# Sparse attention block on one core: tile ends taken in fewer half groups, the mean factor put closer behind its power, and the heaviest tiles summed on the matmul engine alone

## The chip, the cores and the metric

The kernel runs on one core of a Trainium2 chip. The metric is the device time of one execution in microseconds (us), lower is better; the time before is the median of three runs. The trace of one further execution was taken with the hardware profiler.

## The reference, cut to what matters

There are 4096 rows of width 512. Each target row attends only to the source rows that its row of `adj` marks, a few tens at most, with 8 heads of 64.

```python
hs = layer_norm(x, ln1_scale, ln1_bias)
ht = layer_norm(h_target, ln1_scale, ln1_bias)
q = (ht @ Wq + bq).reshape(T, H, HD) / sqrt(HD)
k = (hs @ Wk + bk).reshape(S, H, HD)
v = (hs @ Wv + bv).reshape(S, H, HD)
logits = where(adj != 0, einsum('thd,shd->hts', q, k), NEG)
ctx = einsum('hts,shd->thd', softmax(logits), v).reshape(T, D)
ht = layer_norm(ht + ctx @ Wo + bo, ln2_scale, ln2_bias)
ff = gelu(ht @ W1) @ W2                  # W1: 512x2048, W2: 2048x512
x = _layernorm(x + ht + ff)
```

## The kernel before

**Stages.** Up to about 275 us the kernel projects all source rows to keys and values, stores them as rows of 1024 numbers in the DRAM table `kvd`, and turns the first half of `adj` into lists of neighbours, sorted by length. From then on each of 32 tiles holds 128 target rows of similar neighbour count. A tile's capacity is the longest list in it: the first tile has 11, then come pairs rising to 24; tile 15 has 39 and tile 17 has 38, each paired with a short tile (12 and 13); the pairs after that fall again. Tiles 0 to 15 belong to part 0, tiles 16 to 31 to part 1, whose lists are still built from `adj` while part 0 is being attended to.

**Attention** (`attention`, `values`, `by_scalar`). A tile's neighbours are taken in groups of S = 3 rows. GpSimd (POOL) issues one indirect DMA per row that gathers 128 key-and-value rows from `kvd` into a ring `kv` of 17 rows (20 for part 1). VectorE (DVE) multiplies keys with the query `tq` (L1242), reduces to logits `lg` (L1247) and multiplies two of the three value rows by the probabilities `p` (L1203); ScalarE (ACT) takes the exponential and scales the third row (L1226). From tile ADDS = 11 on DVE adds the second value row to the first (L1207), from tile DENSE = 21 on in every other group also the third (L1210). Each row that is left is added to the context `cps` by four transposing 128x128 matmuls on TensorE (PE, L1214). A slot of the ring comes free when these have read it.

**A tile's end** (`finish`) is a generator. Every group of three is two half groups; in each, `advance` takes one step (up to the next `yield`) of each tile end under way and of each `front` (the gather and projection of a coming tile's query). The steps of an end are: sums and reciprocals, transposes of them (L1117), the product with `cps` (L1122), the output projection `pa` (L1130, L1134), statistics, the variance plus epsilon (L680), its power -0.5 on POOL (L687), the mean factor `nm` (L692) and the normalisation (L1153), and the transposes into `h2T` (L1162, L1166). `turned` notes the tile whose `pa` has been issued, and a coming front may begin once the tile three before it is in `turned`.

**The feed-forward stream** (`feed`) handles one group of one or two tiles at a time. It waits for the group's `h2T`, multiplies by W1 (`pf`, L1348), applies gelu on ACT, multiplies by W2 into `po` (L1357), and hands the group to `end`, which does the last normalisation and stores the rows (L1303 to L1325). Its power also goes to POOL (L1312, L687), and its mean factor is L1318.

**Order.** `_weave` mixes the streams (attention, feed, the lists of part 1, loads of weights) by costs: the stream with the lowest clock goes next and its clock rises by the cost that it yields. Attention and feed have the same total cost per group, so feed runs at attention's pace and stays behind by as much as it was behind when its first `h2T` came. Every engine then runs its own instructions strictly in the resulting order, which the build may still shift a little for each engine.

**Loads of records.** `prefetch` loads a tile's record `rec` (neighbour numbers) on POOL's queue (L998), two tiles ahead.

Of the kernel before, what the change touches and what calls it, by code (L numbers as in the profile page):

```python
# [17 lines left out]
P = 128  # L18
# [360 lines left out]
RW = E0 + RE  # L379
# [64 lines left out]
def adj_resnorm_kernel(  # L444
# [33 lines left out]
    nc = tc.nc  # L478
# [4 lines left out]
    NT = N // P  # L483
# [12 lines left out]
    TILES = [t for g in groups for t in g]  # L496
# [4 lines left out]
    NA, NBT = len(CAPS_A), len(CAPS_B)  # L501
# [11 lines left out]
    recs_d = [dram.tile([n * P, RW], I32, name=f"rec{i}") for i, (_, n) in enumerate(PARTS)]  # L513
# [19 lines left out]
    with tc.tile_pool(name="keep", bufs=1) as keep:  # L533
# [17 lines left out]
        with ExitStack() as late:  # L551
# [126 lines left out]
            def shifted(pool, mv, n, name):  # L678
                ve = pool.tile([P, n], F32, name=name + "_ve")
                nc.vector.tensor_scalar_add(ve, mv[:, :, 1], EPS)  # L680
                return ve
# [13 lines left out]
            def stats(pool, src, mv, name):  # L695
                st = pool.tile([P, 6], F32, name=name + "_st")
                nc.vector.bn_stats(st, src)
                nc.vector.bn_aggr(mv, st)
# [290 lines left out]
            def prefetch(i):  # L989
                if i >= NT or i in recs:  # L990
                    return
                r0 = TILES[i][0]
                part = 1 if r0 >= PARTS[1][0] * P else 0
                assert part in done
                r0 -= PARTS[part][0] * P
                rec = sp.tile([P, E0 + MAXE], I32, name="rec", bufs=6)

                nc.gpsimd.dma_start(rec[:, :RW], recs_d[part][r0:r0 + P, :])  # L998
                recs[i] = rec

            def front(i, idle=0):
# [28 lines left out]
                for kc in range(KC):  # L1030
# [11 lines left out]
            SG = [(i, j0, min(S, cap - j0)) for i, (_, cap) in enumerate(TILES)  # L1042
                  for j0 in range(0, cap, S)]
# [5 lines left out]
                place.append(place[-1] + n)  # L1049

            begun_fronts, turned = set(range(EARLY)), set()
            first_b = next(k for k, (i, _, _) in enumerate(SG) if i >= NA)
            issued = [0]

            def step(gens, i):
# [40 lines left out]
            def finish(i, p, cps, group, hs, mv):  # L1096


                rec, tq, cap = recs[i], tqs.pop(i), TILES[i][1]

                nc.vector.scalar_tensor_tensor(p[:, :cap, :], rec[:, E0:E0 + cap].unsqueeze(2)
                                               .to_broadcast([P, cap, H]), 0.0, p[:, :cap, :],
                                               op0=ALU.is_gt, op1=ALU.mult)
                nc.vector.tensor_reduce(sums[:, i, :], p[:, :cap, :].rearrange("p j h -> p h j"),
                                        AX.X, ALU.add)
                ri = sp.tile([P, H], F32, name="ri")
                nc.vector.tensor_scalar_max(ri, sums[:, i, :], SUM_LO)
                nc.vector.reciprocal(ri, ri)
                rx = sp.tile([P, KC, P], F32, name="rb", bufs=1)
                rxf = rx.rearrange("p c t -> p (c t)")  # L1110
                nc.scalar.copy(rxf.rearrange("p (h d) -> p h d", h=H),
                               ri.unsqueeze(2).to_broadcast([P, H, HD]))
                yield
                yield
                prx = ps.tile([P, KC, P], F32, name="t", bufs=2)
                for c in range(KC):
                    nc.tensor.transpose(prx[:, c, :], rxf[:, c * P:(c + 1) * P], ident)  # L1117
                ct = sp.tile([P, KC, P], F32, name="rb", bufs=1)
                nc.scalar.copy(ct, prx)
                yield  # L1120
                yield
                nc.vector.tensor_mul(ct, cps, ct)  # L1122
                yield
                yield
                yield
                yield
                pa = ps.tile([P, D], F32, name="t", bufs=2)

                for c in range(KC):
                    nc.tensor.matmul(pa[:, c * P:(c + 1) * P], tq[:, D + c * P:D + (c + 1) * P],  # L1130
                                     ident, is_transpose=True, start=c == 0, stop=False,
                                     skip_group_check=True)
                for c in range(KC):
                    nc.tensor.matmul(pa, ct[:, c, :], wo[:, c, :], start=False,  # L1134
                                     stop=c == KC - 1, skip_group_check=True)
                turned.add(i)
                yield
                h = sp.tile([P, D], F32, name="h")
                nc.scalar.copy(h, pa)
                yield  # L1140
                stats(sp, h, mv[:, len(hs), :], "n2")
                hs.append(h)
                if len(hs) < len(group):
                    return
                nh = len(hs)
                ve = shifted(sp, mv[:, :nh, :], nh, "n2")
                yield
                rs = power(sp, mv[:, :nh, :], nh, "n2", ve)
                for _ in range(4):
                    yield  # L1150
                nm = negmean(sp, mv[:, :nh, :], rs, nh, "n2")
                for j, h in enumerate(hs):
                    nc.scalar.activation(h, h, AF.Identity, bias=nm[:, j:j + 1], scale=rs[:, j:j + 1])  # L1153
                yield
                yield
                w = len(hs) * P
                h2T = sp.tile([P, KC, 2 * P], F32, name="h2T")
                for k2 in range(KC // 2):
                    pt = ps.tile([P, 2, 2 * P], F32, name="t", bufs=2)
                    for k in range(2):  # L1160
                        for j, h in enumerate(hs):
                            nc.tensor.transpose(pt[:, k, j * P:(j + 1) * P],  # L1162
                                                h[:, (k2 * 2 + k) * P:(k2 * 2 + k + 1) * P], ident)
                    for k in range(2):
                        kc = k2 * 2 + k
                        nc.scalar.activation(h2T[:, kc, :w], pt[:, k, :w], AF.Identity,  # L1166
                                             bias=b2c[:, kc:kc + 1], scale=s2c[:, kc:kc + 1])
                h2Ts[GROUPS.index(group)] = h2T
# [17 lines left out]
            def attention():  # L1186
# [10 lines left out]
                def values(i, j0, n, kv, p, cps, after):  # L1197

                    m = n - 1 if n == S else n
                    v4 = kv[:, :m, D:].rearrange("p j (h d) -> p j h d", h=H)
                    nc.vector.tensor_tensor(v4, v4, p[:, j0:j0 + m, :].unsqueeze(3)  # L1203
                                            .to_broadcast([P, m, H, HD]), ALU.mult)
                    slots = list(range(n))
                    if m > 1 and i >= ADDS:
                        nc.vector.tensor_add(kv[:, 0, D:], kv[:, 0, D:], kv[:, 1, D:])  # L1207
                        slots.remove(1)
                        if n == S and i >= DENSE and j0 // S % 2:
                            nc.vector.tensor_add(kv[:, 0, D:], kv[:, 0, D:], kv[:, S - 1, D:])  # L1210
                            slots.remove(S - 1)
                    for j in slots:
                        for c in range(KC):
                            nc.tensor.matmul(cps[:, c, :], kv[:, j, D + c * P:D + (c + 1) * P], ident,  # L1214
                                             is_transpose=True, start=j0 + j == 0 and c == 0,
                                             stop=j0 + n == TILES[i][1] and j == slots[-1],
                                             skip_group_check=True)
                    if after is not None:
                        tails.append(after)
# [10 lines left out]
                k = 0  # L1230
                for group in GROUPS:
                    hs = []
                    mv = sp.tile([P, 2, 2], F32, name="mv2")
                    cost = 0.5 * UNIT * len(group) / 2 / sum(TILES[i][1] for i in group)
                    for i in group:
                        cps = ps.tile([P, KC, P], F32, name="cps", bufs=2)
                        while k < len(SG) and SG[k][0] == i:
                            _, j0, n = SG[k]
# [15 lines left out]
                            if pend:  # L1254
                                values(*pend.pop())
                                request(k)
# [41 lines left out]
            def end(group, xs, po):  # L1298
# [14 lines left out]
                yield  # L1313
                rs = power(sp, None, nt, "n3", ve)
                yield
                yield
                nm = sp.tile([P, nt], F32, name="n3_nm")
                nc.vector.tensor_mul(nm, sm[:, :nt, 0], rs)  # L1318
                yield
# [13 lines left out]
            def feed(g):  # L1333
# [5 lines left out]
                fb = 4 // nt  # L1339
                cost = UNIT * nt / 2 / (2 * FC // fb)  # L1340
                xs = []
# [62 lines left out]
            WAIT = 100.0  # L1404
            AHEAD = 4
            ADDS = 11
            DENSE = 21
            UNIT = 60.0

            ed = all_edges()  # L1410
# [107 lines left out]
```

## Time and profile before

| what | value |
|---|---|
| median of three runs | 1790.75 us (1786.41 to 1794.25) |
| profiled execution | 1796.99 us, its span 1795.3 us |
| PE busy | 1660.0 us, 92% of the span |
| DVE busy | 1434.3 us, 80% |
| ACT busy | 1238.7 us, 69% |
| POOL busy | 1049.6 us, 58% |
| last `pa` (tile 31) | starts at 1686.8 us |

The table's busy times are averages over stages with different limits, so the page's share of PE doesn't tell by itself what a change is worth: PE has long idle stretches up to about 1050 us and almost none after it. POOL's instructions that only issue a gather are counted as busy on it; the 0.3 us between two of them are not.

### The profile page before, as it was taken

The page shows a single profiled execution, that of the slowest core. Times are in us where ns is not written, and L with a number is a line of the kernel's source. Part 1 is how long each engine was busy: PE and PEld are TensorE (multiplying, and loading weights), DVE is VectorE, ACT ScalarE, POOL GpSimd, SP SyncE. Part 2 cuts the span into 40 slices and gives each one's busy share as a digit, 9 for nine tenths or more (in the row PEclk, how much of TensorE's full clock was granted, in tenths as well). Part 3 has the DMA queues.
Part 4 walks back from the last instruction along what each step waited for, and adds up shares of the span by engine and source line. Part 5 has one row for each costly group of instructions (what it writes and reads, how often), then busy time and mean ns, then how long its engine had stood idle before and what let it go on. Part 6 is the DMA issues. An engine that isn't in the chain of part 4 may idle for free. (4 is left out here: it accounts for less than half of the span.)

```text
span 1795.3 us, 22273 instructions
## 1 busy us (share of the span) xinstructions
PE 1660.0 (92%) x6746; PEld 1069.5 (60%) x6746; DVE 1434.3 (80%) x2475; ACT 1238.7 (69%) x3129; POOL 1049.6 (58%) x834
## 2 busy tenths in 40 slices
PE   7999985698999899988888899999999999999997
PEld 3444433576676666656556566666666666666664
DVE  6887786899997778968788999998989788979100
ACT  5776663588987686757667687877878778787211
POOL 1000156777656366777788787888777766671101
PEclk9999997799999999999989999999999999999998
DMA  9999978889878687676887677888776776772000
GB/s 354 373 390 361 348 249 317 335 307 353 306 239 295 229 280 270 220 232 208 275 285 254 235 270 270 310 291 292 259 260 235 248 243 228 240 266 75 24 18 26
DMA packets 140265, 460.99 MB, mean 257 GB/s; under 512 B 16500, under 2 KB 21704, under 8 KB 140136
## 3 DMA queue, kind: packets, MB, share of 16 engines
q0 software_dynamic: 96656, 342.51, 55.8%
q1 hardware_dynamic: 35664, 93.88, 14.6%
q10 hardware_dynamic: 7816, 23.08, 3.3%
q8 instruction: 56, 0.92, 0.2%
q14 instruction: 73, 0.60, 0.1%
HBM read 430.61 MB, written 28.79 MB: 256 GB/s over the span
## 5 line engine op out<-in xcount | busy, mean ns | idle before, releaser
L985 POOL DMA_INDIRECT kv<-kvd,rec x603 | 817.3, 1355 | 300.7 <-issue 133.2
L1348 PE MATMUL pf<-h2T,w 128*128 128x256 f32 (+1 forms) x2176 | 470.9, 370 | 1.4 <-ACT h2T L1166 1.4
L1357 PE MATMUL po<-w,gt 128*128 128x512 f32 x1024 | 464.5, 594 | 0.2 <-ACT gt L1351 0.2
L1348 PEld LDWEIGHTS pf<-h2T,w 128*128 128x128 f32 x2176 | 390.8, 192 | 66.3 <-issue 20.0
L1242 DVE TENSOR_TENSOR kv<-kv,tq 128x1536 f32<-128x1536 f32 (+2 forms) x211 | 352.5, 1678 | 57.5 <-DMA kv<-kvd,rec 49.9
L1226 ACT ACTIVATE kv<-kv,pa 128x64 f32<-128x64 f32 x1520 | 393.4, 339 | 4.3
L1247 DVE TENSOR_REDUCE lg<-kv 128x24 f32<-128x1536 f32 (+2 forms) x211 | 351.5, 1670 | 0.5
L1214 PE MATMUL cps<-ident,kv 128*128 128x128 f32 x1724 | 238.1, 284 | 73.0 <-DVE kv L1207 39.2
L1357 PEld LDWEIGHTS po<-w,gt 128*128 128x128 f32 x1024 | 188.4, 191 | 195.4 <-issue 192.9
L1214 PEld LDWEIGHTS cps<-ident,kv 128*128 128x128 f32 x1724 | 208.5, 146 | 154.1 <-DVE kv L1207 57.1
L1203 DVE TENSOR_TENSOR kv<-kv,p 128x1024 f32<-128x1024 f32 (+1 forms) x211 | 251.7, 1194 | 18.9 <-ACT p L1251 17.7
L687 POOL TENSOR_TENSOR n_rs<-n_ve,mhalf 128x2 f32<-128x2 f32 (+2 forms) x51 | 49.9, 978 | 317.6 <-DVE n_ve L680 148.7
L733 ACT ACTIVATE kv<-kv 128x1024 uint8<-128x1024 int32 x128 | 134.6, 1054 | 56.4 <-DMA kv<-in_adj_dram 21.4
L1351 ACT ACTIVATE gt<-pf 128x512 f32<-128x512 f32 x128 | 76.6, 598 | 97.4 <-PE pf L1348 90.2
L1351 ACT ACT_TABLE_LOAD x108 | 138.6, 1283 | 1.8
L1031 PE MATMUL t<-wq,tq 128*128 128x512 f32 x256 | 124.0, 628 | 5.0 <-ACT tq L1024 5.0
L947 PE MATMUL pq<-wv,h2T 128*128 128x512 f32 x256 | 118.3, 606 | 8.1 <-ACT kv L949 4.3
L947 PE MATMUL pq<-wk,h2T 128*128 128x512 f32 x256 | 118.9, 607 | 1.9 <-DMA wk<-in_L_gnn_Wk_dram 1.0
L1134 PE MATMUL t<-wo,rb 128*128 128x512 f32 x256 | 116.2, 592 | 0.0
L742 DVE MAX8 cand<-kv 128x8 uint16<-128x171 uint16 (+1 forms) x384 | 108.3, 326 | 6.9 <-remote 4.8
L1251 ACT ACTIVATE p<-lg 128x24 f32<-128x24 f32 (+2 forms) x179 | 39.4, 220 | 87.2 <-DVE lg L1247 79.8
L1207 DVE TENSOR_TENSOR kv<-kv 128x512 f32<-128x512 f32 x144 | 98.5, 685 | 0.4
(163 smaller groups left out, 1571.2 us busy)
## 6 DMA issues: line engine op xcount, KB each, us to landing
kv<-in_adj_dram SPq DMA_DIRECT2D x128, 512.0 KB
kvd<-tq ACTq DMA_DIRECT2D x23, 512.0 KB
kv<-kvd,rec POOLq DMA_INDIRECT x603
kv<-in_L_gnn_h_target_dram SPq DMA_DIRECT2D x32, 256.0 KB
kv<-in_x_dram SPq DMA_DIRECT2D x15, 512.0 KB
kvd<-kv ACTq DMA_DIRECT2D x9, 512.0 KB
w<-in_L_gnn_W_dram SPq DMA_DIRECT2D x4, 1024.0 KB
w<-in_L_gnn_W_dram ACTq DMA_DIRECT2D x4, 1024.0 KB
```

Source lines behind the costliest of these rows:

```text
L733: nc.scalar.activation(sg, a, AF.Sign, accum_out=dpart[:, i, h:h + 1])
L947: nc.tensor.matmul(pkv, hT[:, kc, j * P:(j + 1) * P], w[:, kc, :], start=kc == 0, stop=kc == KC - 1)
L985: issues[:] = [nc.gpsimd.indirect_dma_start(out=dst, out_offset=None, in_=table[:, :], in_offset=bass.IndirectOffsetOnAxis(ap=idx, axis=0) ...
L1031: nc.tensor.matmul(pq, hT[:, kc, :], wq[:, kc, :], start=kc == 0, stop=kc == KC - 1)
L1203: nc.vector.tensor_tensor(v4, v4, p[:, j0:j0 + m, :].unsqueeze(3) .to_broadcast([P, m, H, HD]), ALU.mult)
L1214: nc.tensor.matmul(cps[:, c, :], kv[:, j, D + c * P:D + (c + 1) * P], ident, is_transpose=True, start=j0 + j == 0 and c == 0, stop=j0 + n ...
L1226: newest[:] = [nc.scalar.mul(v, v, pa[:, hd:hd + 1]).ins]
L1242: nc.vector.tensor_tensor(kv[:, :n, :D], kv[:, :n, :D], tq[:, :D].unsqueeze(1).to_broadcast([P, n, D]), ALU.mult)
L1247: logits[:] = [nc.vector.tensor_reduce(lg[:, :n, :], kv[:, :n, :D].rearrange("p j (h d) -> p j h d", h=H), AX.X, ALU.add).ins]
L1348: nc.tensor.matmul(pf[:, k, :], w1[(f0 + k) // KC][:, kc, (f0 + k) % KC * P:((f0 + k) % KC + 1) * P], h2T[:, kc, :w], start=kc == 0, stop= ...
L1351: nc.scalar.activation(gt, pf, AF.Gelu_apprx_tanh)
L1357: nc.tensor.matmul(po[j], gt[:, k, j * P:(j + 1) * P], w2[(f0 + k) // KC][:, (f0 + k) % KC, :], start=False, stop=f0 + k == FC - 1, skip_g ...
```

## The change

The change has five edits.

1. For the first QUICK = 7 tiles an end's steps come after 1, 1, 1 and 1 half groups where they came after 2, 2, 4 and 2. All other tiles keep 2, 2, 4 and 2.
2. In every end, `nm` comes one half group after the power, not four.
3. In `end`, the mean factor comes one step after the power, not two.
4. Tiles with a capacity of at least HEAVY = 30 (15 and 17) have no additions on DVE: all three value rows of a group go to PE.
5. Records of part 1 are loaded by SyncE (SP) instead of POOL, except for the last four tiles.

An unused name, `first_b`, is removed as well.

```diff
-                nc.gpsimd.dma_start(rec[:, :RW], recs_d[part][r0:r0 + P, :])
+                (nc.sync if part and i < NT - 4 else nc.gpsimd).dma_start(rec[:, :RW], recs_d[part][r0:r0 + P, :])
...
                 rec, tq, cap = recs[i], tqs.pop(i), TILES[i][1]
+                slow = 0 if i < QUICK else 1
...
-                yield
-                yield
+                for _ in range(1 + 1 * slow):
+                    yield
                 prx = ps.tile([P, KC, P], F32, name="t", bufs=2)
...
                 nc.scalar.copy(ct, prx)
-                yield
-                yield
+                for _ in range(1 + 1 * slow):
+                    yield
                 nc.vector.tensor_mul(ct, cps, ct)
-                yield
-                yield
-                yield
-                yield
+                for _ in range(1 + 3 * slow):
+                    yield
                 pa = ps.tile([P, D], F32, name="t", bufs=2)
...
                 rs = power(sp, mv[:, :nh, :], nh, "n2", ve)
-                for _ in range(4):
-                    yield
+                yield
                 nm = negmean(sp, mv[:, :nh, :], rs, nh, "n2")
                 for j, h in enumerate(hs):
                     nc.scalar.activation(h, h, AF.Identity, bias=nm[:, j:j + 1], scale=rs[:, j:j + 1])
-                yield
-                yield
+                for _ in range(1 + 1 * slow):
+                    yield
...
-                    if m > 1 and i >= ADDS:
+                    if m > 1 and i >= ADDS and TILES[i][1] < HEAVY:
                         nc.vector.tensor_add(kv[:, 0, D:], kv[:, 0, D:], kv[:, 1, D:])
...
                 rs = power(sp, None, nt, "n3", ve)
                 yield
-                yield
                 nm = sp.tile([P, nt], F32, name="n3_nm")
...
+            HEAVY = 30
             DENSE = 21
+            QUICK = 7
```

More of the change, by code (lines that the diff above doesn't have):

```diff
@@ L1051, in adj_resnorm_kernel @@
             begun_fronts, turned = set(range(EARLY)), set()
-            first_b = next(k for k, (i, _, _) in enumerate(SG) if i >= NA)
             issued = [0]
```

## The prediction

> **What bounds the kernel now.** I read the busy time by stage first, then the end of PE's timeline for prices, then POOL's and DVE's timelines around the powers.
>
> ```profile
> core 0: us, PE busy (x) PEld busy (x) DVE busy (x) ACT busy (x) POOL busy (x), PEclk, DMA share, GB/s
> 340.00:605.00 265.00, 245.84 (x1185) 173.59 (x1184) 237.00 (x397) 210.04 (x554) 171.28 (x137) 0.97 0.82 290
> ...
> 776.00:945.00 169.00, 142.07 (x585) 96.92 (x585) 133.75 (x154) 110.03 (x308) 135.31 (x105) 0.91 0.76 253
> 945.00:1022.00 77.00, 67.34 (x292) 43.47 (x291) 68.82 (x70) 57.10 (x159) 62.35 (x39) 1.00 0.72 239
> ...
> 1050.00:1119.00 69.00, 67.27 (x289) 42.95 (x287) 67.53 (x70) 57.49 (x161) 56.46 (x40) 1.00 0.75 260
> 1119.00:1687.00 568.00, 562.05 (x2342) 374.81 (x2342) 483.14 (x597) 425.78 (x1099) 385.83 (x296) 1.00 0.70 236
> 1687.00:1795.00 108.00, 95.64 (x395) 62.89 (x393) 6.49 (x25) 18.02 (x34) 10.58 (x12) 0.96 0.06 21
> ```
>
> The cuts at 605, 945, 1022, 1050, 1119 and 1687 are where `pa` of tiles 7, 14, 15, 16, 17 and 31 runs, so 945 to 1022 and 1050 to 1119 are the two heavy tiles. After 1687 PE is alone with feed-forward matmuls that were left over. PE's timeline prices them:
>
> ```profile
> 1743.69 3.62 PE L1348 MATMUL pf<-h2T,w 128*128 128x256 f32 x16
> 1747.14 7.03 PE L1357 MATMUL po<-w,gt 128*128 128x512 f32 x16
> 1754.01 7.31 PE L1348 MATMUL pf<-h2T,w 128*128 128x128 f32 x64
> 1761.15 0.60 PE L1382 MATMUL po<-ident,h2T 128*128 128x128 f32 x4
> ```
>
> From start to start a record costs 0.216 us at 256 columns (3.45/16), 0.43 at 512 (6.87/16), 0.11 at 128 (7.14/64). At these prices the records of 1119 to 1687 add up to 566 of 568 us: **PE is the bound there**, and a matmul added or saved counts in full. Earlier PE has slack: 19.7 us of recorded idle in 340 to 605 (mainly 5.1 waiting for L1203 at 341, 5.0 for ACT's L1017 at 409, 5.9 for ACT's L1024 at 584), 36 us against the prices in 776 to 945, 9 in tile 15, 3 in tile 17.
>
> In 776 to 945 the bound is **POOL's queue**: 105 instructions busy for 135.3 us with 0.3 us between two make 167 of 169 us.
>
> ```profile
> 843.44 0.61 POOL L998 DMA_DIRECT2D rec<-rec  x1
> 844.35 0.98 POOL L985 DMA_INDIRECT kv<-kvd,rec  x1 [0.30 <-issue]
> ...
> 848.13 1.98 POOL L985 DMA_INDIRECT kv<-kvd,rec  x1 [0.30 <-issue]
> ...
> 851.86 0.74 POOL L687 TENSOR_TENSOR n_rs<-n_ve,mhalf 128x2 f32<-128x2 f32 x1
> ```
>
> ```profile
> 845.43 0.15 DVE L680 TENSOR_SCALAR n_ve<-mv 128x2 f32<-128x2 f32 x1
> ...
> 857.10 0.16 DVE L692 SCALAR_TENSOR_TENSOR n_nm<-mv,n_rs 128x2 f32<-128x2 f32 x1 [6.08 <-POOL n_rs L687]
> ```
>
> A record load costs the queue 0.91 us (843.44 to 844.35). A power stands in the queue behind gathers: here 11.6 us pass from the variance on DVE to the end of the second power, and DVE stands still for 6.1 of them.
>
> **What the Trainium skill says.** "SBUF — State Buffer", section "Who interferes with whom": a DVE instruction with two SBUF inputs contends with a GpSimd instruction that reads SBUF. The trace agrees: of 646 gathers between 300 and 1640 us 236 took over 1.3 us where the median is 0.96, and these spend 42% of their time under L1242, 26% under L1203 and 9% under L1207, the short ones 10, 8 and 6%. "DMA: Bandwidth & Descriptors", section "SWDGE vs HWDGE vs iDMA": a DMA issued from SP has its descriptors made by hardware and doesn't use GpSimd. No run here shows a record load on SP yet.
>
> **The change, part by part.** Where instructions move I counted in the order of the two built programs.
>
> *Quick ends (edit 1).* The first feed-forward matmul comes after 24 rows of context instead of 33, about 341 us instead of 357.7. Priced as above, the feed-forward work done before a tile's `pa` is 14 us against 0 at tile 1, 69 against 48 at tile 4, 190 against 155 at tile 8, 345 against 317 at tile 14; what is left after the last `pa` falls from 89.9 to 69.2 us. That is no gain in itself. The tail loses 20.7 us, but the same matmuls now stand before `pa` of tile 31, and where PE is full they push attention back by as much. The gain is the idle time that they fill, at most the 19.7 us of 340 to 605. The two waits for ACT (10.9 us) belong to fronts of coming tiles, which now begin sooner because `turned` is set sooner; half of the 5.1 us can be filled from 341 on. I take **-13**. Bounds: -19 (all filled) and +5, since DVE is busy 237 of 265 us there and can itself be held up by matmuls put before its inputs.
>
> *The mean factor (edits 2 and 3).* This adds a wait: DVE's work between variance and mean factor is the cover for POOL's power. For groups 5 to 10 it falls from 7.5, 4.2, 7.6, 10.4, 7.8, 3.7 us to 0.9, 2.5, 4.4, 3.0, 1.4, 1.4; in `end`, for groups 6, 7, 9, 10, from 35, 27, 26, 21 us to 4.7, 1.4, 0.2, 0.2. Powers took 2.0, 11.6, 8.6, 11.5, 11.1, 2.3 us and 12.2, 18.4, 6.4, 9.7 us. If these stood, DVE would stall some 20 + 40 = 60 us more. Queued behind the waiting instruction are the next groups' L1242 and the query L1036, and PE's L1214 waits for those. Two things soften it. The powers now stand behind fewer gathers (rows issued ahead of DVE in `end` of groups 6 and 7: 11 and 9, not 17), and at 1.65 us a row (1.355 + 0.3) the shorter queue takes off 10 to 13 us. And a stall passes on only in part: when DVE stood 8.3 us at 1408, PE's recorded idle in 1366 to 1448 was 2.1 us, a quarter. Left are 16 us in groups 9 and 10, where 17 rows stay ahead: **+3 to +4**, bounds 0 and +30 (60 us, half passed on). Nothing is gained where the factor comes sooner, as the feed stream is still busy with the group before; in the last six groups the factor of `finish` was at most 1.9 us of work behind already.
>
> *Heavy tiles (edit 4).* 26 additions of 0.685 us leave DVE (17.8 us), 104 transposing matmuls of 0.109 us come to PE (11.3 us, 5.7 a tile). Tile 17 has 66.4 us of matmuls in 69, so at least 3.1 us longer, at most 5.7: +4. Tile 15 has 67.7 in 77: DVE is busy 68.8 and waits 8.2 for gathers, so it loses 7.8 and its gathers are held up less; between -3.6 (down to 73.4 of matmuls) and +5.7, I take -2. Together **+2**, bounds -0.5 and +11.3.
>
> *Records (edit 5).* 12 loads of 0.91 us leave POOL; 5 of them stood between 843 and 923, where POOL is the bound: 4.6 us. SP's last other transfer was issued at 698 us, so nothing is behind them there. I take **-3**, bounds -4.6 and 0. The other seven lie where PE is the bound: nothing.
>
> ACT gets 4 more table loads of 1.28 us, hidden in its 31% of idle time. The last chain (L1305 to the store, 3.8 us) stays. Sum: -13 + 3 + 2 - 3 = -11 us. The profiled execution took 1796.99, 6.2 over the median, so it would be 1786; on the median of 1790.75 it is **1780**.
>
> **Rivals.**
>
> *Powers take the gain (slower).* One mechanism: L692 and L1318 wait on DVE for a power behind full-ring gathers. For it: the latencies of 9 to 18 us in 845 to 1166, and DVE busy 67.5 of 69 us in tile 17, where nothing hides a stall. Against: the quarter passed on at 1408. It decides once more than 11 us reach PE; with 60 us stalled and half passed on it is -13 + 30 + 2 - 3 = +16, about 1807.
>
> *The early work only moves the gap (same).* In the new order group 0's feed-forward is packed into rows 24 to 33 and then none stands until row 50, 17 rows against 15 before. At 2.07 us a row (30 rows in 402 to 464) DVE needs 35 us for these, PE's matmuls 26, so up to 9 us of new idle. Then the early part gives -3 and the whole -1: about 1790. For it: DVE at 89% in that stretch. Against: DVE can run ahead in the ring while PE works off the packed part.
>
> *The change doesn't do what it says.* The build shifts instructions, so steps need not move by the half groups written. The counted orders speak against it.
>
> **How the numbers follow.** A measurement of this kernel can tell about 0.5% (9 us) from no change. The likeliest case, -11, gets 0.48 for faster; with the early idle all filled, no stall and the low ends of the other two (-19 + 0 - 0.5 - 4.6) it reaches down to 1767, and the three runs spread 4 us below their median: 1763. The packed gap and mixtures around zero get 0.27 for same; the powers, or heavy tiles at their full 11.3 us with an early part of nothing, get 0.25 for slower. The range of 1763 to 1804 holds the first two and the nearer half of the last.
>
> **What would show it right or wrong.** In the profile after: the first `pf` near 341; PE's idle in 340 to 605 well under 20 us and no waits for L1017 or L1024; some 69 us between the last `pa` and the end of `po`; tile 17 some 4 us longer and no wait of PE for L1207 in tiles 15 and 17; DVE's waits for L687 up from 30.4 us (all L692) but PE idle after 1119 still under 10. Wrong: a gap of 9 us or more between groups 0 and 1, or waits of PE for L1203 behind powers of more than 11 us in sum.

## The result, and the profile after

The changed kernel takes 1786.4 us (median of 13 runs, 1782.4 to 1792.4). The kernel before took 1792.6 us in 13 runs beside it (1786.4 to 1800.1). The ratio is **0.9966, interval 0.9951 to 0.9980**: about 6 us faster, roughly half of the 11 us forecast. The same kernel measured again later (run g0_changed_again) gave 0.9984 [0.9968, 1.0000], so the gain is 3 to 6 us, and the second interval touches no change. The profiled execution of the changed kernel took 1783.65 us (span 1781.9), 2.7 below its median, and that of before 1796.99, 4.3 above its own; so 7 of the 13.4 us between the two profiles are scatter between executions.

The busy time by stage of the changed kernel, with most cuts where `pa` of tiles 7, 14, 15, 16, 17 and 31 runs (the columns are in the first line):

```profile
core 0: us, PE busy (x) PEld busy (x) DVE busy (x) ACT busy (x) POOL busy (x), PEclk, DMA share, GB/s
340.00:624.00 284.00, 271.03 (x1265) 188.06 (x1264) 233.37 (x394) 213.00 (x549) 167.44 (x137) 0.98 0.76 264
...
793.00:951.00 158.00, 137.70 (x601) 94.58 (x601) 131.51 (x138) 109.73 (x308) 126.28 (x102) 0.94 0.81 269
951.00:1023.00 72.00, 70.75 (x337) 49.40 (x336) 62.80 (x69) 58.92 (x158) 50.01 (x42) 1.00 0.81 273
...
1047.00:1122.00 75.00, 71.84 (x332) 49.24 (x331) 61.37 (x68) 55.49 (x153) 59.96 (x45) 0.98 0.86 288
1122.00:1696.00 574.00, 560.54 (x2309) 372.61 (x2308) 483.53 (x591) 425.64 (x1098) 373.68 (x284) 0.99 0.68 226
1696.00:1782.00 86.00, 74.21 (x316) 48.49 (x314) 4.59 (x18) 13.37 (x25) 5.90 (x7) 0.94 0.04 14
```

Read the first two numbers of a row against each other. PE's idle time in the first row is 13.0 us (before 19.2). The heavy tiles are nearly full (1.3 and 3.2 us idle). In 1122 to 1696 it is 13.5 us, where before had 6: **the stage where PE was the bound has acquired idle time**. The last row, from `pa` of tile 31 to the end, is down from 108 to 86 us. The first feed-forward matmul comes at

```profile
336.96 7.41 PE L1344 MATMUL pf<-h2T,w 128*128 128x128 f32 x64 [0.33 <-ACT h2T L1163]
```

instead of at 357.7. (Lines of the changed kernel stand three or four lower: L1200, L1204, L1211, L1239, L1314, L1344, L1353 are the earlier L1203, L1207, L1214, L1242, L1318, L1348, L1357.) What PE waited for in the stage after tile 17, in total, times and longest us:

```profile
PE t L1159 <- DVE tq L1036: 8.3, 2, 4.2
PE cps L1211 <- DVE kv L1204: 4.0, 4, 2.2
```

Before, the second of these (4.1 us there) was nearly all it had. The first is new, and DVE's waits for the power say where it begins. Over the whole span they were, first in the kernel before and then in the changed one:

```profile
DVE n_nm L692 <- POOL n_rs L687: 30.4, 21, 8.3
DVE n_nm L692 <- issue: 7.4, 2, 4.2
DVE n_nm L1318 <- POOL n_rs L687: 2.5, 3, 0.9
```

```profile
DVE n_nm L692 <- POOL n_rs L687: 40.1, 27, 7.8
DVE n_nm L1314 <- POOL n_rs L687: 5.2, 5, 1.8
```

The row that the profile puts down to "issue" is a wait for the power too: both of its waits end 0.03 us after a power does. So over the whole span the waits grew by only 5 us (40.3 to 45.3). What changed is where they stand: from `pa` of tile 17 on they grew from 20.8 to 32.9 us.

One such place can be followed through three timelines of the changed kernel. POOL first, then DVE, then PE:

```profile
1338.11 0.94 POOL L985 DMA_INDIRECT kv<-kvd,rec  x1 [0.30 <-issue]
1339.07 0.73 POOL L687 TENSOR_TENSOR n_rs<-n_ve,mhalf 128x2 f32<-128x2 f32 x1
```

```profile
1330.63 0.17 DVE L680 TENSOR_SCALAR n_ve<-mv 128x2 f32<-128x2 f32 x1
1331.31 0.69 DVE L1204 TENSOR_TENSOR kv<-kv 128x512 f32<-128x512 f32 x1
...
1339.84 0.16 DVE L692 SCALAR_TENSOR_TENSOR n_nm<-mv,n_rs 128x2 f32<-128x2 f32 x1 [7.84 <-POOL n_rs L687]
...
1346.37 0.68 DVE L1036 SCALAR_TENSOR_TENSOR tq<-t,bqr 128x512 f32<-128x512 f32 x1
```

```profile
1342.32 0.60 PE L1159 MATMUL t<-ident,h 128*128 128x128 f32 x4
1347.11 1.12 PE L1159 MATMUL t<-ident,h 128*128 128x128 f32 x4 [4.19 <-DVE tq L1036]
1348.58 5.65 PE L1344 MATMUL pf<-h2T,w 128*128 128x256 f32 x16
1354.28 3.62 PE L1344 MATMUL pf<-h2T,w 128*128 128x256 f32 x16
```

The variance is ready at 1330.8, but the power on POOL ends at 1339.8, behind gathers. DVE, in order, stands 7.84 us at L692, and everything behind it is late, among it the query L1036. L1036 still reads one of the two PSUM buffers `t`, so PE's next transposes into `t` (L1159) stand 4.19 us. The first 16 feed-forward matmuls after that idle time take 5.65 us, the next 16 take 3.62: another 2 us.

### The profile page after: what moved, and what is told of

Same layout as the page of the kernel before. It is cut to its first block, busy times and chain, and to the rows that moved or that the text cites. A ratio compares the mean times of both kernels' runs of the same rounds, so it can differ in the third digit from the quotient of the medians.

```text
span 1781.9 us, 22463 instructions
## 1 busy us (share of the span) xinstructions
PE 1666.0 (93%) x6850; PEld 1078.9 (61%) x6850; DVE 1425.0 (80%) x2449; ACT 1240.4 (70%) x3133; POOL 1018.9 (57%) x822
## 3 DMA queue, kind: packets, MB, share of 16 engines
q1 hardware_dynamic: 37392, 94.06, 14.9%
## 5 line engine op out<-in xcount | busy, mean ns | idle before, releaser
L985 POOL DMA_INDIRECT kv<-kvd,rec x603 | 795.4, 1319 | 335.4 <-issue 118.5
L1344 PE MATMUL pf<-h2T,w 128*128 128x256 f32 (+1 forms) x2176 | 474.5, 372 | 4.5 <-ACT h2T L1163 4.5
L1353 PE MATMUL po<-w,gt 128*128 128x512 f32 x1024 | 463.7, 594 | 0.0
L1344 PEld LDWEIGHTS pf<-h2T,w 128*128 128x128 f32 x2176 | 393.0, 193 | 74.3 <-issue 20.3
L1239 DVE TENSOR_TENSOR kv<-kv,tq 128x1536 f32<-128x1536 f32 (+2 forms) x211 | 351.1, 1675 | 55.6 <-DMA kv<-kvd,rec 52.0
L1353 PEld LDWEIGHTS po<-w,gt 128*128 128x128 f32 x1024 | 187.6, 191 | 194.5 <-issue 193.1
L1211 PEld LDWEIGHTS cps<-ident,kv 128*128 128x128 f32 x1828 | 217.6, 144 | 121.5 <-issue 41.8
L1211 PE MATMUL cps<-ident,kv 128*128 128x128 f32 x1828 | 244.1, 280 | 50.1 <-DVE kv L1200 32.1
L1200 DVE TENSOR_TENSOR kv<-kv,p 128x1024 f32<-128x1024 f32 (+1 forms) x211 | 251.1, 1192 | 25.8 <-ACT p L1248 24.4
L733 ACT ACTIVATE kv<-kv 128x1024 uint8<-128x1024 int32 x128 | 134.4, 1052 | 53.4 <-DMA kv<-in_adj_dram 21.8
L1132 PE MATMUL t<-wo,rb 128*128 128x512 f32 x256 | 121.0, 615 | 8.1 <-DVE rb L1122 8.1
L1031 PE MATMUL t<-wq,tq 128*128 128x512 f32 x256 | 116.8, 600 | 1.3 <-ACT tq L1024 1.3
L947 PEld LDWEIGHTS pq<-wv,h2T 128*128 128x128 f32 x256 | 48.9, 193 | 66.8 <-issue 57.5
```

The lines of the kernel that those rows point to most:

```text
L733: nc.scalar.activation(sg, a, AF.Sign, accum_out=dpart[:, i, h:h + 1])
L947: nc.tensor.matmul(pkv, hT[:, kc, j * P:(j + 1) * P], w[:, kc, :], start=kc == 0, stop=kc == KC - 1)
L985: issues[:] = [nc.gpsimd.indirect_dma_start(out=dst, out_offset=None, in_=table[:, :], in_offset=bass.IndirectOffsetOnAxis(ap=idx, axis=0) ...
L1239: nc.vector.tensor_tensor(kv[:, :n, :D], kv[:, :n, :D], tq[:, :D].unsqueeze(1).to_broadcast([P, n, D]), ALU.mult)
L1344: nc.tensor.matmul(pf[:, k, :], w1[(f0 + k) // KC][:, kc, (f0 + k) % KC * P:((f0 + k) % KC + 1) * P], h2T[:, kc, :w], start=kc == 0, stop= ...
L1353: nc.tensor.matmul(po[j], gt[:, k, j * P:(j + 1) * P], w2[(f0 + k) // KC][:, (f0 + k) % KC, :], start=False, stop=f0 + k == FC - 1, skip_g ...
```

## The experiments

Each ratio is to the kernel before on the same chip, with its interval in the text. "Slack" is a stage's length minus its matmuls at the prices of the prediction (0.109, 0.216, 0.43 us), every record counted once. No record is missing: each kernel without edit 4 has 6746 and each with it 6850, the prediction's 104 more. Each stage is from one execution, so differences of 2 or 3 us are not read. Stages run from `pa` to `pa` of the tiles named; lengths are in brackets where they matter; the tail is the length from `pa` of tile 31 to the end of the last `po`. The expectations give the slack after tile 17 some 9 us lower throughout (2, 15 and 38 us for the kernel before, the changed one and a2), since some records are counted twice in their sums; their differences agree with the table's. The last column is the time that DVE waited for powers at the two lines of the mean factor from `pa` of tile 17 on.

| kernel | ratio | 271 us to tile 7 | 11-14 | 14-17 | 17-31 | tail | waits |
|---|---|---|---|---|---|---|---|
| before | 1 | 68.6 | 38.3 (163.5) | 20.3 (173.6) | 11.6 (568.0) | 96.1 | 20.8 |
| changed | 0.9966 | 59.1 | 25.8 (152.8) | 7.9 (171.6) | 24.7 (573.3) | 74.5 | 32.9 |
| changed again, g0 | 0.9984 | 61.7 | 25.6 (152.6) | 9.8 (173.6) | 27.3 (575.8) | 74.5 | 35.4 |
| a1, edit 1 alone | 0.9977 | 54.5 | 34.5 (159.7) | 16.5 (169.8) | 28.0 (576.6) | 82.3 | 45.5 |
| a2, edits 2 and 3 alone | 1.0059 | 66.4 | 33.8 (162.5) | 14.4 (171.6) | 46.5 (599.8) | 78.0 | 43.8 |
| a4, edit 4 alone | 0.9991 | 68.8 | 34.9 (162.7) | 13.2 (176.1) | 10.0 (565.5) | 96.1 | 23.2 |
| a5, edit 5 alone | 0.9985 | 71.6 | 40.3 (165.6) | 15.1 (168.4) | 14.9 (571.3) | 96.1 | 23.6 |
| b1, changed, no edit 1 | 1.0006 | 64.0 | 24.5 (155.8) | 16.3 (176.6) | 22.2 (581.2) | 78.0 | 41.0 |
| b2, changed, no edits 2 and 3 | 0.9969 | 54.3 | 29.1 (156.1) | 15.1 (178.9) | 21.8 (569.5) | 82.3 | 45.1 |
| d1, changed, late factors late again | 1.0007 | 62.6 | 27.8 (155.7) | 21.9 (182.2) | 17.5 (568.6) | 82.3 | 33.4 |
| c2, before, no powers | 0.9894 | 66.0 | 31.9 (157.1) | 11.6 (167.5) | 10.9 (564.7) | 96.1 | 0 |
| c1, changed, no powers | 0.9796 | 56.9 | 25.3 (152.2) | 8.2 (172.0) | 7.1 (555.7) | 74.5 | 0 |
| f2, before, all roots on DVE | 0.9918 | 67.2 | 31.9 (157.1) | 18.2 (172.4) | 7.2 (562.7) | 96.1 | 0 |
| f1, changed, all roots on DVE | 0.9891 | 56.4 | 26.9 (153.9) | 10.6 (174.4) | 13.5 (562.1) | 74.5 | 0 |
| g1, changed, late roots on DVE | 0.9918 | 59.0 | 25.4 (152.4) | 10.9 (174.7) | 8.9 (557.5) | 74.5 | 0 |
| g2, all roots on DVE, no edit 4 | 0.9826 | 53.1 | 25.3 (149.7) | 11.1 (165.3) | 10.1 (559.6) | 74.5 | 0 |

My theory after seeing the result was that the powers, put at +3 to +4 in the sum, cost more than that after tile 17. Rivals: the early part gained less than 13, or the heavy tiles cost more than 2.

**The parts alone: a1, a2, a4, a5.** Each is the kernel before with the edits named, copied from the diff shown above.

a1: 

> The kernel before with edit 1 alone (ends of the first seven tiles in fewer half groups). Counted in its order, 76 us of feed-forward are left after the last pa (90 before, 69 with all edits), and the first end of tile 0 is as early as with all edits but its mean factor is not. Theory of the sum (early idle filled, -13 for the whole change): most of it shows here, -7 to -12 us, with PE's recorded idle between 340 us and pa of tile 7 down by 5 us or more. Rival 1 (the gap only moves): -2 to +2 us. Rival 2 (powers take the gain): also waits of DVE for L687 up, because the covers in `end` fall here too (from 26, 21, 18 us to 2 or 3 in groups 9 to 11): +2 to +6.

Measured: 0.9977 [0.9960, 0.9993], 4.1 us faster, between the ranges of the theory and of rival 1. The slack up to tile 7 fell by 14 us and the tail by 14, but the stage after tile 17 took on 16 us of slack, with DVE waiting there 45.5 us for powers (before 20.8). The early gain is real and is lost later, and edits 2 and 3 are not needed for the loss.

a2: 

> The kernel before with edits 2 and 3 alone (mean factor one step after its power, in every end and in `end`). The recorded prediction took it as a pure cost of +3 to +4. Counted in its order it leaves 73 us of feed-forward after the last pa, so it makes the feed stream start sooner nearly as much as edit 1 does. Theory of the prediction: +3 to +4 us. Revised theory (it is also an early start): -3 to -8 us, first pf before 352 us. Rival (powers take the gain): +5 us or more, DVE's waits for L687 over 50 us and PE's idle after pa of tile 17 over 15 us.

Measured: 1.0059 [1.0028, 1.0090], some 10 us slower. The windows view of a2 after tile 17 (columns as in the first windows view above):

```profile
1122.00:1722.00 600.00, 570.80 (x2320) 377.69 (x2319) 482.08 (x595) 417.88 (x1094) 388.17 (x293) 0.97 0.65 218
```

PE is idle for 29 of 600 us there; before it was idle for 6. That is the rival's case and not the revised theory's. But the tail fell from 96 to 78 us: counted in order, the feed-forward work left after the last `pa` is 73 us, where before left 90. A mean factor that comes sooner lets the feed start sooner, and that lead stays to the end.

a4: 

> The kernel before with edit 4 alone (no additions on DVE in tiles 15 and 17). Theory of the sum: +2 us (tile 15 some 2 us shorter, tile 17 some 4 longer). Rival (PE pays in full): +8 to +11 us, with both tiles longer by 5 us. Rival (DVE and POOL were the bound of both tiles): -2 to -6, with tile 15 shorter by over 4 us.

Measured: 0.9991 [0.9970, 1.0012]; tile 15 went from 77.7 to 75.7 us and tile 17 from 68.4 to 76.2, the short tile between them from 27.5 to 24.2.

a5: 

> The kernel before with edit 5 alone (records of part 1 loaded by SP, but for the last four tiles). The order of PE and DVE is that of before. Theory of the sum: -3 us, the stretch between pa of tile 11 and pa of tile 14 shorter by 3 to 5 us. Rival (POOL's time comes back as waits for the ring): 0 us. Rival (a record arrives later by SP, and gathers wait for it): +2 us or more.

Measured: 0.9985 [0.9969, 1.0002], 2.7 us. The time agrees with the -3 forecast, though the interval touches no change; the stage 11-14, where it should show, is not shorter in this profile (165.6 against 163.5 us). In the changed kernel SP issues the loads; where the prediction had 0.91 us of POOL's queue for each, SP's timeline says

```profile
853.83 15.63 SPq L998 DMA_DIRECT2D rec<-rec  x4
...
917.30 0.32 SPq L998 DMA_DIRECT2D rec<-rec  x1
```

one issue takes 0.32 us (the first row is four issues and what lay between them).

**One part left out: b1, b2, b4.** These are the changed kernel without edit 1, without edits 2 and 3, and without edit 4.

b1: 

> The changed kernel without edit 1, so edits 2 to 5. If the edits add up (edits 2 and 3 alone measured +0.59%), this stands at about +0.35%. If instead edit 2 only hurts while the kernel's other ends are as they were, and records and heavy tiles take its harm away, it stands at -0.2 to +0.1%. The slack of PE after pa of tile 17 was 2 us before, 15 in the changed kernel, 38 with edits 2 and 3 alone: expected here 30 to 40 if it is edit 2 in the late tiles that makes it, under 20 if it is the early start.

Measured: 1.0006 [0.9990, 1.0022]. Without the quick ends nothing is gained. The time is where the expectation put it if edits 4 and 5 take away the harm that edits 2 and 3 do alone, and the slack after tile 17 is 22.2 us, 11 more than before, where a2 had 46.5. That is under the bound that the expectation set for the early start (20 there, 29 at the table's count). How edits 4 and 5 take the harm away is not shown.

b2: 

> The changed kernel without edits 2 and 3 (mean factors as before), so edits 1, 4 and 5. If the edits simply add up (edit 1 alone measured -0.23%, edit 4 -0.09%, edit 5 -0.15%), this stands at -0.47%, 2 to 3 us better than the changed kernel. Theory (the power waits after pa of tile 17 take the early gain, and they come with every earlier start of the feed stream): PE's slack after pa of tile 17 is as large as with edit 1 alone, 13 to 17 us, and the time -0.2 to -0.5%. Rival (the mean factors are needed for the gain): slower than the changed kernel by 3 us or more, that is above -0.15%.

Measured: 0.9969 [0.9952, 0.9985], the same as the whole (0.9966, 0.9984). Edits 2 and 3, which alone cost 0.6%, cost nothing in the whole. The edits do not add: the four singles sum to +0.1%. And the waits for powers are there without edits 2 and 3. From 1125 us on DVE waited in b2:

```profile
DVE n_nm L692 <- POOL n_rs L687: 32.7, 6, 7.8
DVE n_nm L1317 <- POOL n_rs L687: 12.4, 9, 2.9
```

The slack after tile 17 is 21.8 us, 10 more than before and about 3 to 5 less than in the whole. So leaving out edits 2 and 3 takes away only a small part of what the changed kernel lost there.

b4: 

> The changed kernel without edit 4 (DVE's additions in tiles 15 and 17 back). Theory (heavy tiles cost about what they bring: edit 4 alone measured -0.09 +- 0.2%): within 3 us of the changed kernel, -0.2 to -0.5% against before. Rival (the 11.3 us of extra matmuls are paid in the full change, since PE is fuller there): 6 to 10 us better than the changed kernel, -0.7 to -0.9%. Rival (additions and power waits together make DVE the bound of both tiles): 5 us worse, about 0.

Measured: 1.0010 [0.9992, 1.0028]. So edit 4 would be worth about 0.3 to 0.4% inside the changed kernel, against 0.1 +- 0.2% alone. This was unexpected; a repetition stands below.

**No powers: c1, c2.** In `power`, for the ends' n2 and n3:

```diff
-nc.gpsimd.tensor_tensor(rs, ve, mhalf[:, :n], ALU.pow)
+nc.vector.tensor_scalar(rs, ve, 1.0, None, op0=ALU.mult)
```

c1 is the changed kernel with this, c2 the kernel before with it.

c1: 

> The changed kernel, but the power of the ends isn't computed: in its place DVE copies the variance in one small operation, so no end waits for POOL (the normalised rows are therefore not those of the reference; nothing else is left out). Theory (DVE's waits for powers in POOL's queue cost the second half some 10 us): -8 to -14 us against the changed kernel, about -0.8 to -1.1% against before, PE's slack after pa of tile 17 under 6 us. Rival (the slack there comes from where the feed stream's matmuls fall in the order, not from the powers): within 4 us of the changed kernel, slack still over 10 us.

c2: 

> The kernel before with the same cut: DVE copies the variance instead of waiting for POOL's power in the ends. DVE waited 31 us for powers in the kernel before. Theory (the waits of the kernel before were nearly all hidden, since PE's slack after pa of tile 17 is 2 us): 0 to -5 us. Rival (powers cost before as much as after): -8 us or more, so that the change doesn't make them worse.

Measured: c1 0.9796 [0.9766, 0.9826], c2 0.9894 [0.9872, 0.9917]. POOL's powers cost about 19 us in the kernel before (1.06% of 1792) and about 30 in the changed one (0.9966 - 0.9796 = 1.7%): **11 us more**, within about 7 by the intervals. Both expectations were too small: -8 to -14 us for c1, 0 to -5 for c2. The stages say where the cost stands. In the kernel before most of it comes ahead of tile 17: only 3 of c2's gain are after it (568.0 to 564.7). In the changed kernel it is nearly all after tile 17 (573.3 and 575.8 to 555.7), where c1 has less slack, 7.1 us, than c2 with 10.9. Without powers the change adds no slack there and would be worth about 1% (0.9796/0.9894 = 0.990).

**The root on DVE: f1, f2, g1.** These approximate the same power on DVE, with eight small operations and two Newton steps, instead of POOL's one:

```python
def root(pool, ve, n, name):
    h = pool.tile([P, n], I32, name=name + "_h")
    nc.vector.tensor_single_scalar(h, ve.bitcast(I32), 1, op=ALU.logical_shift_right)
    y = pool.tile([P, n], F32, name=name + "_rs")
    nc.vector.tensor_scalar(y.bitcast(I32), h, -1.0, float(0x5f3759df), op0=ALU.mult, op1=ALU.add)
    t = pool.tile([P, n], F32, name=name + "_t")
    for _ in range(2):
        nc.vector.scalar_tensor_tensor(t, y, -0.5, y, op0=ALU.mult, op1=ALU.mult)
        nc.vector.tensor_mul(t, t, ve)
        nc.vector.scalar_tensor_tensor(y, t, 1.5, y, op0=ALU.add, op1=ALU.mult)
    return y
```

f1 is the changed kernel with `root` in all ends, f2 the kernel before with it, g1 the changed kernel with it only in ends from tile 15 on.

f1: 

> The changed kernel with the power of the ends computed on DVE itself: eight small operations (a shift, a subtraction and two Newton steps) instead of one on POOL; all results are computed. Without any power the changed kernel stood at -2.04% against before. Eight small operations for 33 powers are some 30 us of DVE, about half of it where DVE has 85 us of idle time. Theory (it is the wait in POOL's queue that costs, not the power): -1.4 to -1.9%, PE's slack after pa of tile 17 under 6 us. Rival (DVE is too full for it): -0.3 to -0.9%, no better than 10 us under the changed kernel.

f2: 

> The kernel before with the same roots on DVE. Without any power it stood at -1.06%. Theory: -0.5 to -0.9%, so that the change is worth 0.8 to 1.1% (14 to 19 us) once no end waits for POOL, twice what it is worth with the waits. Rival (the change is worth 6 us whatever the powers do): within 0.4% of the changed kernel with roots on DVE.

g1: 

> The changed kernel with roots on DVE for the ends of the groups that end with tile 16 and later (in `end`: whose first tile is 15 or later), powers on POOL for the earlier ones. All results are computed. Theory (the late waits for powers are the missing term): 8 to 14 us better than the changed kernel, PE's slack after pa of tile 17 under 6 us, the stages up to tile 14 as in the changed kernel; with the early DVE spared it is as good as roots everywhere (-1.09%) or better, -0.9 to -1.4%. Rival (roots gain mostly by emptying POOL's queue in the stretch of tiles 11 to 14): less than 5 us better than the changed kernel.

Measured: f1 0.9891 [0.9859, 0.9924], f2 0.9918 [0.9886, 0.9951], g1 0.9918 [0.9892, 0.9943]. Between f2 and f1 the change is worth 0.27%, not the 0.8 to 1.1% expected of it once no end waits for POOL; this is what f2's rival said (the change is worth 6 us whatever the powers do). The roots are not free: against the kernels without powers they cost the changed kernel 0.95% (0.9891 - 0.9796) and the kernel before 0.24% (0.9918 - 0.9894), and f1 keeps 6 us more slack after tile 17 than f2. g1 is the sharper test of the late waits: it touches late ends only, is 12.0 us below the changed kernel run again, g0 (1775.84 and 1787.83), and its slack after tile 17 falls from 27.3 to 8.9 us. Some 3 us of these 12 can be waits that the kernel before had there too, by c2. The same place in g1's DVE timeline:

```profile
1331.83 0.21 DVE L680 TENSOR_SCALAR n_ve<-mv 128x2 f32<-128x2 f32 x1
...
1332.56 0.21 DVE L685 TENSOR_SCALAR n_h<-n_ve 128x2 int32<-128x2 int32 x1
...
1335.05 0.16 DVE L705 SCALAR_TENSOR_TENSOR n_nm<-mv,n_rs 128x2 f32<-128x2 f32 x1
```

From variance to mean factor it is 3.2 us with other work between, without a stall, where the changed kernel took 9.2 us (1330.63 to 1339.84). With PE waiting no more, the stage after tile 17 is full, as g1's windows view shows:

```profile
1128.00:1686.00 558.00, 553.98 (x2308) 366.68 (x2307) 495.64 (x703) 425.18 (x1097) 360.00 (x270) 1.00 0.69 233
```

**Where the factor must come soon: d1.** The changed kernel with edit 3 undone and edit 2 kept for the first seven tiles only:

```diff
-                yield
+                for _ in range(1 + 3 * slow):
+                    yield
                 nm = negmean(sp, mv[:, :nh, :], rs, nh, "n2")
```

d1: 

> The changed kernel with edit 2 kept for the first seven tiles only and edit 3 undone: mean factors of later ends four half groups behind their powers again. The feed stream is as early as in the changed kernel up to tile 8. Theory (late mean factors close behind their powers cost the second half): -0.5 to -0.9%, 4 to 8 us better than the changed kernel. Rival (the build packs the mean factors close behind the powers anyway; counted in its order DVE's work between variance and factor is still 1 to 4 us for most ends after tile 15): within 3 us of the changed kernel.

Measured: 1.0007 [0.9992, 1.0022], not the 4 to 8 us gained that the theory expected. The slack after tile 17 is smaller (17.5 us), but tile 15 took 87.7 us where the changed kernel took 72.6, and b2, which lacks the same edits there, 81.2. PE's timeline of this kernel in that tile:

```profile
982.07 0.47 PE L1161 MATMUL t<-ident,h 128*128 128x128 f32 x1 [4.36 <-ACT h L1152]
...
994.33 1.11 PE L1021 MATMUL t<-ident,tq 128*128 128x128 f32 x4 [7.24 <-ACT h2T L1165]
```

The feed has caught up with the ends, and PE waits for `h` and `h2T`: beside the early start, a later mean factor is a cost in that place. It isn't the only thing that makes tile 15 long: b1, which has the soon factors and not edit 1, took 81.0 us, and a1, which has edit 1 and not the soon factors, 72.8.

**The heavy tiles again: g0, g2, g3.** g0 is the changed kernel, g3 is b4 again, g2 is b4 with `root` in all ends.

g0: 

> The changed kernel once more, beside the next three on the same chip. Expected -0.34% against before (-0.2 to -0.49%), PE's slack after pa of tile 17 between 12 and 18 us. If it stands at 0, the -0.34% of its first timing was a matter of the chip.

g3: 

> The changed kernel without edit 4, once more, beside the changed kernel. First measured at +0.10% against before, 0.44% over the changed kernel. Theory (edit 4 about even): within 0.25% of the changed kernel of this call. Rival (edit 4 is worth 8 us in the changed kernel): 0.3 to 0.6% above it, and then a stage of tiles 14 to 17 or one after it longer by several us.

g2: 

> The changed kernel without edit 4 and with roots on DVE everywhere. With edit 4 that kernel stood at -1.09%. Theory (edit 4 relieves DVE, which the roots load): -0.6 to -0.9%. Rival (edit 4 is about even, as it measured alone): -0.9 to -1.2%. Rival (the 11 us of extra matmuls are paid): -1.4% or better.

Measured: g0 0.9984 [0.9968, 1.0000], g3 0.9993 [0.9973, 1.0013], g2 **0.9826 [0.9800, 0.9852]**. Over both pairs edit 4 is worth 0.1 to 0.4% in the changed kernel; g3 alone can't be told from g0. With the root on DVE its sign turns: without it the kernel is 0.65% faster (0.9826 against f1's 0.9891), and the stage 14-17 takes 165.3 instead of 174.4 us, about the 11.3 us of its matmuls. In g3, which has the additions on DVE again, tile 17 (80.2 us, 75.7 in the changed kernel) shows a wait on PE and two on DVE (first fence PE's timeline, second DVE's):

```profile
1055.55 0.59 PE L1346 MATMUL pf<-h2T,w 128*128 128x256 f32 x2
...
1062.37 1.97 PE L1213 MATMUL cps<-ident,kv 128*128 128x128 f32 x8 [6.23 <-DVE kv L1206]
```

```profile
1056.57 1.76 DVE L1241 TENSOR_TENSOR kv<-kv,tq 128x1536 f32<-128x1536 f32 x1 [6.35 <-DMA kv<-kvd,rec]
...
1072.86 0.16 DVE L692 SCALAR_TENSOR_TENSOR n_nm<-mv,n_rs 128x2 f32<-128x2 f32 x1 [5.34 <-POOL n_rs L687]
```

DVE waits for a gather until 1056.57, and PE waits for the addition that follows at 1061; DVE's wait for a power comes later in the same tile. I read this as tile 17 having slack on PE only as long as DVE is held up by POOL; a kernel that removes just the gather's wait was not made, so this part is argued and not shown.

g2, at 1760.3 us, is 27 us below the changed kernel and 31 below the kernel before that ran beside it.

## Why the prediction was right or wrong

The sign and the range held; the size, -11, was about twice what was measured or more. The step that failed is the one on the waits for powers: they were charged to edits 2 and 3 alone, at +3 to +4, and edit 1 was charged none. After tile 17 they cost PE 13 to 16 us more than before, and 10 of that stay when edits 2 and 3 are left out.

That the total came no further off is in part luck. Up to tile 11 the slack fell by 3 to 8 us where -13 was forecast, and after tile 17 it grew by 13 to 16 where +3 was; but tiles 11 to 17 became 11 to 13 us shorter where the sum had -1. Step by step:

- **Quick ends, -13: too large, and the mechanism right only in part.** The first `pf` came 20.7 us sooner and the tail shrank by 21.6 us, as counted. The slack up to tile 7 fell by 7 to 10 us in the two profiles of the changed kernel and by 14 in a1, but from tile 7 to 11 it rose by 1 to 6 (from 7.9 us; this stage isn't in the table). The waits for L1017 and L1024 are gone from 340 to 624; waits for L1200 (7.4 us) and L1132's input (3.2) stand in their place, most of them in the gap between the first two groups (below).
- **Waits for powers, +3 to +4: this term failed.** The slack after tile 17 went from 11.6 to 24.7 and 27.3 us. That the powers make it is shown: without them the change adds none (c1 7.1, c2 10.9, and 11 us between the two costs), and g1, without the late ones, has 8.9. Three parts of the working failed. *Which edit:* a1, with edit 1 alone, has 45.5 us of waits and 28.0 of slack there; b2, without edits 2 and 3, has 45.1 and 21.8, and the same time as the whole. So an earlier feed stream brings the waits, whichever edit makes it earlier; the prediction priced no wait under edit 1. Counted in a1's order, DVE's work between variance and mean factor falls with edit 1 too, in `end` (26, 21, 18 us to 2 or 3); but most of a1's waits are at L692 (34.3 of 45.5 us), and why those grow is not shown. *Where:* the 16 us were to come in `end` for groups 9 and 10 (now L1314), but in the changed kernel that line waited only 5.2 us over the whole span; the stalls are at L692. *How it passes on:* a quarter was taken, from the one stall at 1408. Against the kernel before, slack grew by 13.1 us with 12.1 us more of waits in the changed kernel, by 16.4 with 24.7 in a1, 10.2 with 24.3 in b2, 5.9 with 12.6 in d1, 34.9 with 23.0 in a2. So in these single executions the share ran from 0.4 to 1.5, and no fixed one holds. In the place followed above DVE's late query holds a PSUM buffer of PE, and the matmuls after the idle time run slower.
- **What stays open.** With every root on DVE the change is worth 0.27% (f1 against f2, each within 0.33%), without any power 1.0%. I read the difference as DVE's room, which the eight operations take up in the fuller order; no run separates this.
- **"Nothing is gained where the factor comes sooner": wrong beside edit 1, open alone.** d1, which takes the soon factors from the late tiles, is 0.2 to 0.4% slower than the changed kernel, with 87.7 us for tile 15 against 72.6. But b2, without any of them, is as fast as the whole, and a2, with them alone, leaves 73 us of feed-forward after the last `pa` instead of 90 and is slower.
- **Heavy tiles, +2.** Alone, tiles 14 to 17 took 2.5 us longer in a4's profile and the ratio was within 0.2% of none, as forecast: tile 15 gave 2.0 back, tile 17 took 7.8, above the +4, and the short tile between gave 3.3. PE's wait for L1207 in tile 15 (9.6 us before) fell to 0.2 in the changed kernel. In the changed kernel the edit gains 0.1 to 0.4% (b4, g3), which the sum did not have.
- **Records, -3: agrees in size** (a5), within an interval of -5.5 to +0.4 us that doesn't exclude none. In the changed kernel the stage 11-14 shortened by 10.7 us, more than a1 (-3.8), a2 (-1.0), a4 (-0.8) and a5 (+2.1) give alone. It doesn't hold fewer matmuls: at the prices 127.0 us against 125.2. POOL, whose queue was the bound, was busy 122.7 us there against 132.0: 3.0 are the five record loads, and as many gathers of `kv` (75 and 74) took 5.7 less. Why these were shorter stays open.
- **The rivals.** The slower one, powers behind gathers, did happen, with 13 to 16 us at PE, above its point of decision (11), and at L692, which it names; the earlier stages and the tail outweighed it. The packed gap happened in part: between the last `po` of group 0 and the first `pf` of group 1 PE was idle for 10.4 us (10.0 in g0), where before had 5.7, in pieces of at most 5.4. This is one reason why the early part fell short of 13. That the change doesn't do what it says is excluded by the traces.
- **The prices.** The 566 of 568 us in the prediction are about 10 too high for the same reason as in the expectations; with every record counted once the matmuls from `pa` of tile 17 to that of tile 31 make 556, and the slack is 11.6. The reading that PE is the bound there stands on its idle time, 6 us of 568.

## What to carry to other kernels

A small operation put on an engine whose queue is full of transfers has to be priced by its queue, not by its length: in the place followed here a power of 0.73 us came 9.0 us after its input. The 34 powers of the ends cost 19 to 30 us of the kernel's time in sum, and moving them to the engine that needs them gained more (0.8%, f2) than the whole change did. Price such a wait under every edit that moves work ahead of it, and not only under the edit that touches it. How much of a stall the next engine feels is no fixed share: follow the stalled engine's later instructions to the buffers that they hold. Edits that move work against each other do not add: run the whole minus one part as well as one part alone.

## What the runs showed that I had not expected

- Sixteen matmuls of 256 columns took 5.65 us after 4.19 us of idle PE and 3.62 us in the next block; so the wait cost about 6 us, not 4. The granted clock of the 6 us from 1347.11 on was 0.55. The same followed all seven idle times of PE over 2.6 us after 340 us in the changed kernel: the next 9 us, further idle time apart, held 1.4 to 3.4 us less of matmuls at the prices than they could. In the kernel before, idle times of 2.65 and 3.20 us (ending at 971 and 992) were not followed by it, with a clock of 1.00.
- Eight dependent operations on 128x2 tiles on DVE cost 0.16 to 0.21 us each and, from variance to mean factor, 3.2 us with other work between, while DVE's one wait for POOL cost 7.84 us in the same place.
